# Natural forms of three weights by 32-column block loads and VectorE transposes, in place of TensorE transposes; a fixed order around the chain's head

## The chip, the cores and the metric

The kernel runs on one core of a Trainium2 chip. The metric is the device time of one execution in microseconds (us); a version is measured in several runs, and the median counts. The profile is of one execution: each instruction on TensorE (PE, and PEld for its weight loads), VectorE (DVE), ScalarE (ACT), GpSimd (POOL) and SyncE (SP, which issues most transfers), and every DMA packet.

## The reference, cut to what matters

Four layers on an image of 8 x 512 x 32 x 32, all in float32. The first layer has f, g and h as 1x1 convolutions with batch statistics, and a spectral norm for each image; the second is an attention over the 1024 points of an image.

```python
# layer 0
f = relu(batchnorm(conv1x1(x, Wf, bf)))      # 64 channels; statistics over all 8 images
g = relu(batchnorm(conv1x1(x, Wg, bg)))
h = conv1x1(x, Wh, bh)
z = einsum('bcn,bcm->bnm', f, g)             # per image
attn = z / largest_singular_value(z)
x = conv1x1(einsum('bnm,bcm->bcn', attn, h), Wv, bv) + x
# layer 1
h = group_norm(x)
q, k, v = wq @ h + bq, wk @ h + bk, wv @ h + bv        # wq, wk, wv, wp: 512 x 512
attn = softmax(q.T @ k * 512 ** -0.5)
x = x + wp @ (v @ attn.T) + bp
# layer 2: a second attention with 128 channels; layer 3: signs of x times signs of W, batch norm, PReLU
```

The kernel doesn't make q and k. It uses `q.T @ k = h.T (wq.T wk) h`, so it makes the product `wu` of the two weights once, and likewise `wo` from wv and wp. The host hands every weight over with its input channel on the partitions ("turned"); the products `wu` and `wo` need wq, wk and wv the other way round, with the output channel on the partitions. These are the natural forms of this document.

## The kernel before

**First stage (`for b in range(B)`, line 1360).** For each image its tile `xt` (2 MB, four quarters `cc` of 512 KB) is loaded on SP's queue into one of two buffers, so the load of image b waits until TensorE has read image b-2. TensorE makes f, g and h (line 1372, `bank<-xt,fg` and `bank<-xt,h`), ScalarE evicts f, VectorE evicts g and takes statistics of both (`bn_stats`). For the last two images h is left for later (`late_h`). Between the images the table `later` (line 1347) loads the other weights: w3 beside image 1, q beside 2, k beside 3, v beside 4, z and tpg beside 6, each as one DMA; the scheduler places them in SP's queue.

**Natural forms (`natural`, line 1332).** A generator. For each weight TensorE turns 16 blocks of 128x128 with the identity into two wide PSUM tiles; ScalarE and VectorE evict them, four blocks of 128 at a time. q is turned behind the last image's f and g, k around the statistics, v as the first thing that `filler` gives.

**Statistics.** Two aggregates on VectorE, then a matmul with `fold` (line 1517) for the mean over images, small VectorE work, a second matmul with `fold` (line 1523) for the variance, `rsqrt_eps` (GpSimd's power and a Newton step on VectorE), and the scale and bias of the ReLU (`relu`, line 1502, on ScalarE). Each f goes to DRAM (`f_dram`) and comes back later (`load_f`).

**Grams.** For a pair of images `turned_pair` turns f and g with TensorE (line 1266) and evicts half with VectorE, half with ScalarE; `gram` (line 1473) makes their 64x64 products.

**The chain (`first_chain`, line 1147).** The singular value of the first pair by repeated squaring: 22 steps, each two matmuls of 128x128 (lines 1159, 1160) whose evictions (one VectorE, one ScalarE) the next step needs, and in every third step a total (line 1187). Between the steps TensorE takes pieces of other work from the generator `filler` (line 1577), a fixed number for each step: first the turning of v, then the product `wu` (line 1417, 16 pieces; its first half evicted by ScalarE, its second by VectorE), the late h of two images, the grams of the other pairs with VectorE's sums of `wu` (`sums_u`) and the bias products (line 1451) among them, and last the product `wo`. The ReLUs of the other images are put on ScalarE one per step.

**Entering image 6.** Seven stages of `enter` (line 419) with 2, 2, 2, 2, 4, 3 and 6 pieces of `filler` between them: `weights0` (line 299), four visits of matmuls (line 429) that VectorE adds to x with statistics, a matmul with `gmat` (line 450), another (line 457), whose result gives the scale of h. Then h is made (`normal`, line 480), and the main part starts with line 405.

**Order.** TensorE's instructions in the loop of the chain stand under `tc.manual_schedule`: they keep the order in which the program gives them. What stands ahead of it, from the statistics to the first two grams, is ordered by the scheduler.

Of the kernel before, what the change touches and what calls it, by code (L numbers as in the profile page):

```python
# [8 lines left out]
F32 = mybir.dt.float32  # L9
# [3 lines left out]
ALU = mybir.AluOpType  # L13
# [3 lines left out]
P = 128  # L17
B = 8
C = 512
N = 1024  # L20
CC = C // P
# [39 lines left out]
COL = {n: 4 * i for i, n in enumerate(VEC512)}  # L61
# [6 lines left out]


NSTEP = 6  # L70

# [12 lines left out]
def kernel(  # L86
# [17 lines left out]
    nc = tc.nc  # L104
    mm = nc.tensor.matmul
# [11 lines left out]
    def wide():  # L117
        return psum["wide"].tile([P, N], F32, tag="wide", name="wide")
# [4 lines left out]
    def bank():  # L123
        return psum["bank"].tile([P, HF], F32, tag="bank", name="bank")
# [25 lines left out]
    sbw = {}  # L150

    def load_w(name, src, shape, pool=wpool, eng=nc.sync, tag=None):
        t = pool.tile(shape, F32, tag=tag or name, name=name)
        eng.dma_start(out=t, in_=src)
        sbw[name] = t
        return t
# [4 lines left out]
    a1 = early.enter_context(tc.tile_pool(name="a1", bufs=1))  # L161
# [32 lines left out]
    fold = fold.rearrange("p g j -> p (g j)")  # L194
# [1134 lines left out]

    nat = {}  # L1330

    def natural(name, tag):
        t = nat[name] = a1.tile([P, CC, C], F32, tag=tag, name="nat_" + name)
        for i in range(CC // 2):
            tp = wide().rearrange("p (o c j) -> p o c j", o=2, j=P)
            for k in range(2):
                for cc in range(CC):
                    nc.tensor.transpose(
                        tp[:, k, cc, :], sbw[name][:, cc, bass.ts(2 * i + k, P)], ident
                    )  # L1340
            dst = t[:, 2 * i : 2 * i + 2, :].rearrange("p o (c j) -> p o c j", j=P)
            nc.scalar.copy(dst[:, 0], tp[:, 0])
            nc.vector.tensor_copy(dst[:, 1], tp[:, 1])
            yield


    later = {
        1: [("w3", w_3, a1)],
        2: [("q", w_q, a1)],
        3: [("k", w_k, a1)],  # L1350
        4: [("v", w_v, a1)],
        6: [("z", w_z, wpool), ("tpg", w_tpg, wpool)],
    }
    shapes = {"z": [P, C], "tpg": [P, CC, 3 * P]}
# [5 lines left out]
    for b in range(B):  # L1360
        xt = load_x(b) if b else first
        for name, src, pool in later.get(b, ()):
            load_w(name, src, shapes.get(name, [P, CC, C]), pool)
        if b == 4:
            load_rows()
        if b >= B - 2:
            resident[b] = xt
        banks = [bank() for _ in w0[: 3 if b < B - 2 else 2]]

        def products(i, cc):  # L1370
            for h in range(NH):
                mm(  # L1372
                    out=banks[i][side(h), :],
                    lhsT=w0[i][:, cc, :],
                    rhs=xt[:, cc, half(h)],
                    start=cc == 0,
                    stop=cc == CC - 1,
                )

        if b == 0:  # L1380
            for cc in range(CC):
                for i in range(2):
                    products(i, cc)
        for i in range(3):
            if i == 2 and b >= B - 2:
                if b == B - 1:
                    for _ in natural("q", "w3"):
                        pass
                continue
            if b or i == 2:  # L1390
                for cc in range(CC):
                    products(i, cc)
            if i == 0:
                nc.scalar.copy(fs[b], banks[i])
                nc.vector.bn_stats(st[:, 0, b, :], fs[b])
            elif i == 1:
                nc.vector.tensor_copy(gs[b], banks[i])
                nc.vector.bn_stats(st[:, 1, b, :], gs[b])
                if last is not None:
                    turn(last[0], last[1], ht_pair[last[0] // 2], 0)  # L1400
        if b < B - 2:
            hraw = a2.tile([P, HF], F32, tag="hraw", name="hraw")
            nc.scalar.activation(hraw, banks[2], AF.Identity, bias=bhc)
            last = b, hraw
        else:
            last = None
        if b == 3:
            total3 = sign_weights()
        if b == 5:
            scale_signs(total3)  # L1410

    def product(lt, rhs, dst, vector):
        for i in range(CC // 2):
            ps = wide()
            for k in range(2):
                for oc in range(CC):
                    mm(  # L1417
                        out=ps[:, half(k)],
                        lhsT=lt[:, oc, bass.ts(2 * i + k, P)],
                        rhs=rhs[:, oc, :],  # L1420
                        start=oc == 0,
                        stop=oc == CC - 1,
                    )
                    if k == 0 or oc < CC - 1:
                        yield
            to = dst[:, 2 * i : 2 * i + 2, :].rearrange("p o c -> p (o c)")
            if i % 2 and vector:
                nc.vector.tensor_copy(to, ps)
            else:
                nc.scalar.copy(to, ps)  # L1430
            yield
# [70 lines left out]
    def relu(b, i):  # L1502
        t = (fs, gs)[i][b]
        nc.scalar.activation(t, t, AF.Relu, bias=bi0[:, i : i + 1], scale=sc0[:, i : i + 1])
        if i == 0:
            nc.sync.dma_start(out=f_dram[b], in_=t)


    mv = a1.tile([P, 2, 2], F32, tag="mv", name="mv")
    mean = a1.tile([P, 2], F32, tag="mean", name="mean")  # L1510
    dev = a1.tile([P, 2], F32, tag="dev", name="dev")
    for i in range(2):
        nc.vector.bn_aggr(mv[:, i, :], st[:, i, :, :])
    nat_k = natural("k", "q")
    next(nat_k)
    ps = bank()
    mm(out=ps[:, 0:2], lhsT=fold, rhs=mv[:, :, 0], start=True, stop=True)
    nc.vector.tensor_copy(mean, ps[:, 0:2])
    nc.vector.tensor_tensor(dev, mv[:, :, 0], mean, ALU.subtract)
    nc.vector.tensor_tensor(dev, dev, dev, ALU.mult)  # L1520
    nc.vector.tensor_tensor(dev, dev, mv[:, :, 1], ALU.add)
    ps = bank()
    mm(out=ps[:, 0:2], lhsT=fold, rhs=dev, start=True, stop=True)
    sc0 = rsqrt_eps(a1, ps[:, 0:2], 2, "r0")
    bi0 = a1.tile([P, 2], F32, tag="bi0", name="bi0")
    m0 = a1.tile([P, 2], F32, tag="m0", name="m0")
    c0 = COL["L0_conv_bf"]
    bias, gamma, beta = (ct[:, c0 + 2 * i : c0 + 2 * i + 2] for i in range(3))
    nc.vector.tensor_tensor(sc0, sc0, gamma, ALU.mult)
    nc.vector.tensor_tensor(m0, mean, bias, ALU.add)  # L1530
    nc.vector.tensor_tensor(bi0, bias, m0, ALU.subtract)
    nc.vector.tensor_tensor(bi0, bi0, sc0, ALU.mult)
    nc.vector.tensor_tensor(bi0, bi0, beta, ALU.add)
    jl = order[0] // 2
    for i in range(2):
        for k in range(2):
            relu(2 * jl + k, i)
    next(nat_k)

    def sums_u():  # L1540

        a11, a12, a21, a22 = quarters_of(wu, chunks, cols2)
# [34 lines left out]
    def filler():  # L1577

        yield from natural("v", "k")
        load_w("p", w_p, [P, CC, C], a1, tag="v")
        yield from product(nat["q"], nat["k"], wu, True)
        for b in order[:2]:
            yield from late_h(b)
        yield from gram(jl, 2, ht_pair[jl], gtl)
        scale_z()
        yield
        between = biases()
        sums = sums_u()  # L1590
        for j in rest:
            for _ in grams(j):
                next(sums, None)
                yield
                if next(between, None):
                    yield
        yield from product(nat["v"], sbw["p"], wo, False)

    todo = filler()
    for _ in range(5):  # L1600
        next(todo)
    for ftl, gtl in turned_pair(jl):
        pass
    for i, t in ((0, ftl), (1, gtl)):
        for _ in gram(jl, i, t, t):
            next(todo)

    relus = iter([(2 * j + k, i) for j in rest for i in range(2) for k in range(2)])
    with tc.manual_schedule(engines={mybir.EngineType.PE}):
        steps = entering(0)  # L1610
        for k, _ in enumerate(first_chain(jl)):

            for _ in range(4 if k == 3 * NSTEP + 3 else 2 if k % 3 == 1 or k == 0 else 1):
                next(todo, None)
            for args in (next(relus, None),):
                if args:
                    relu(*args)
        for n in (2, 2, 2, 2, 4, 3, 6):
            next(steps)
            for _ in range(n):  # L1620
                next(todo, None)
        for _ in todo:
            pass
# [194 lines left out]
```

## Time and profile before

| | |
|---|---|
| median of 3 runs | 1878.11 us (1877.98 to 1878.81) |
| the profiled execution, its whole time | 1878.7 us |
| its span, first to last instruction | 1876.8 us |
| granted TensorE clock | 0.999 of full speed |
| TensorE, 87.9 to 95.6 us | busy 6.80 of 7.70 us |
| TensorE, 105.0 to 150.7 us | busy 42.46 of 45.70 us |
| TensorE, 150.7 to 172.2 us | busy 21.50 of 21.50 us |
| VectorE, 38.3 to 49.4 us | busy 2.58 of 11.10 us |
| issue of x tiles 2, 3, 4, 5 on SP | at 17.19, 28.24, 39.28, 50.32 us |
| TensorE begins x tiles 3, 4, 5 | at 39.07, 50.11, 61.14 us |

The span is 1.9 us shorter than the execution's time, which holds what lies around the program. A line of a timeline has the start and the length in us, the engine, the line of the program, the operation, the tiles that it writes and reads, its shapes and how many instructions stand together; in brackets the idle time of the engine before it, and what ended it. A float32 matmul is shown as two records. A table by stretch has for each its length, the busy time of the five engines with the number of instructions, the clock, the share of the 16 DMA engines that were busy, and GB/s.

### The profile page before, as it was taken

How to read it: one execution, taken by the hardware profiler on the slowest of the kernel's cores; microseconds unless marked ns; L12 is line 12 of the kernel's file. 1: busy time of each engine (PE TensorE's matmuls, PEld its weight loads, DVE VectorE, ACT ScalarE, POOL GpSimd, SP SyncE). 2: the span in 40 equal slices, each digit the busy share in tenths (PEclk: the TensorE clock that was granted, in tenths of full speed). 3: DMA queues.
4: the chain of work that ended last, by engine and by line, in shares of the span. 5: the costliest groups of instructions: out<-in, count | busy, mean ns of one | idle time of the engine just before them, and what ended most of it. 6: DMA issues, size and time to landing. Idle time of an engine off the chain costs nothing.

```text
span 1876.8 us, 16564 instructions
## 1 busy us (share of the span) xinstructions
PE 1856.3 (99%) x6244; PEld 952.5 (51%) x6244; DVE 1118.4 (60%) x2077; ACT 545.4 (29%) x888; POOL 121.9 (6%) x109
## 2 busy tenths in 40 slices
PE   9999999999999999999999999999999999999997
PEld 3456465544645455544645455544645464544653
DVE  3347687467754777567764676457643666355447
ACT  2142221244202521244202522144202521244113
POOL 1000001100020001100020001100020001000011
PEclk9999999999999999999999999999999999999999
DMA  8420000002000200002000200001000200000001
GB/s 323 164 79 7 1 18 1 1 34 73 12 1 12 90 18 1 0 34 73 12 1 12 88 19 0 1 34 67 12 0 12 90 12 0 1 34 23 12 0 47
DMA packets 25202, 66.51 MB, mean 35 GB/s; under 512 B 3552, under 2 KB 4764, under 8 KB 24476
## 3 DMA queue, kind: packets, MB, share of 16 engines
q1 hardware_dynamic: 24188, 64.96, 9.6%
q8 instruction: 51, 0.84, 0.2%
q10 hardware_dynamic: 864, 0.43, 0.1%
q14 instruction: 35, 0.29, 0.0%
q0 software_dynamic: 64, 0.00, 0.0%
HBM read 46.44 MB, written 18.94 MB: 35 GB/s over the span
## 4 chain that ended last, share of the span: by engine, by line
PE 96%; DVE 2%; ACT 1%; DMA 0%; issue 0%; POOL 0%; DVEq 0%; ACTq 0%
PE bank L405 46%; PE bank L583 21%; PE bank L832 6%; PE bank L985 5%; PE bank L1372 4%; PE bank L684 3%; PE bank L701 3%; PE bank L429 2%; PE bank L724 1%; PE wide L1417 1%; PE bank L1053 1%; PE bank L1473 1%; PE bank L855 0%; PE quad L1266 0%; PE bank L1563 0%; PE bank L1159 0%
## 5 line engine op out<-in xcount | busy, mean ns | idle before, releaser
L583 PE MATMUL bank<-e,vt 128*128 128x512 f32 x768 | 336.2, 594 | 0.0
L583 PEld LDWEIGHTS bank<-e,vt 128*128 128x128 f32 x768 | 144.3, 190 | 172.3 <-issue 167.9
L405 PE MATMUL bank<-ut,h 128*128 128x512 f32 x384 | 178.9, 597 | 0.0
L405 PEld LDWEIGHTS bank<-ut,h 128*128 128x128 f32 x384 | 71.3, 190 | 94.7 <-issue 93.0
L405 PE MATMUL bank<-us,hs 128*128 128x512 f32 x256 | 115.6, 593 | 0.0
L832 PE MATMUL bank<-tpg 128*128 128x512 f32 x256 | 115.4, 595 | 0.0
L985 PE MATMUL bank<-e,tpg 128*128 128x512 f32 x256 | 114.7, 595 | 0.0
L356 DVE TENSOR_TENSOR e<-bank,e 128x512 f32<-128x512 f32 x96 | 66.1, 689 | 60.8 <-PE bank L405 45.1
L839 ACT ACTIVATE e<-bank 128x512 f32<-128x512 f32 x128 | 76.3, 597 | 67.0 <-PE bank L832 67.0
L350 ACT COPY e<-bank 128x512 f32<-128x512 f32 x96 | 56.2, 585 | 118.8 <-PE bank L405 118.5
L405 PE MATMUL bank<-wo,h 128*128 128x256 f32 x384 | 89.9, 384 | 0.0
L405 PE MATMUL bank<-h,wu 128*128 128x512 f32 x192 | 88.9, 594 | 0.0
L985 PEld LDWEIGHTS bank<-e,tpg 128*128 128x128 f32 x256 | 48.1, 190 | 60.4 <-issue 60.0
L236 POOL TENSOR_TENSOR r_r<-r_v,minus_half 128x4 f32<-128x4 f32 (+1 forms) x11 | 10.9, 989 | 1044.9 <-DVE r_v L235 1039.3
L405 PEld LDWEIGHTS bank<-wo,h 128*128 128x128 f32 x384 | 71.4, 190 | 12.6 <-issue 3.8
L405 PEld LDWEIGHTS bank<-us,hs 128*128 128x128 f32 x256 | 48.4, 190 | 57.5 <-issue 54.5
L844 DVE TENSOR_TENSOR esum<-esum,e 128x1024 f32<-128x1024 f32 x48 | 58.8, 1226 | 30.1 <-ACT e L839 29.9
L712 ACT ACTIVATE sg<-xt,rb 128x512 f16<-128x512 f32 x64 | 44.2, 716 | 107.9 <-DVE xt L703 105.0
L832 PEld LDWEIGHTS bank<-tpg 128*128 128x128 f32 x256 | 47.6, 190 | 55.0 <-issue 52.4
L356 DVE TENSOR_TENSOR vt<-bank,vt 128x512 f32<-128x512 f32 x48 | 33.2, 692 | 66.4 <-PE bank L405 65.5
L350 ACT COPY vt<-bank 128x512 f32<-128x512 f32 x64 | 37.3, 584 | 121.3 <-PE bank L405 121.2
L350 ACT COPY ut<-bank 128x512 f32<-128x512 f32 x48 | 28.1, 586 | 126.9 <-PE bank L405 126.9
(370 smaller groups left out, 2926.4 us busy)
## 6 DMA issues: line engine op xcount, KB each, us to landing
xt<-in_x SPq DMA_DIRECT2D x55, 512.0 KB
out<-both SPq DMA_DIRECT2D x63, 256.0 KB
rfull<-r_dram SPq DMA_DIRECT2D x15, 512.0 KB
f_dram<-f SPq DMA_DIRECT2D x8, 256.0 KB
fb<-f_dram SPq DMA_DIRECT2D x8, 256.0 KB
w<-in_w SPq DMA_DIRECT2D x1, 1024.0 KB
q<-in_w_q SPq DMA_DIRECT2D x1, 1024.0 KB
k<-in_w_k SPq DMA_DIRECT2D x1, 1024.0 KB
```

The lines of the kernel that those rows point to most:

```text
L350: nc.scalar.copy(dst, ps)
L356: nc.vector.tensor_tensor(dst, ps, u, ALU.add)
L405: mm(out=ps[:, q * w : (q + 1) * w], lhsT=lt(ka, kb, q, k), rhs=rhs(ka, kb, q, k), start=first and q == 0 and k == 0, stop=last and k == 1 ...
L583: mm(out=ps, lhsT=a[:, t, bass.ts(r_, P)], rhs=e[t], start=first and t == 0, stop=last and t == NTH - 1, skip_group_check=True,)
L684: mm(out=ps[:, i, :], lhsT=xt[:, cc, bass.ts(4 * h + i, P)], rhs=sbw["tpg"][:, cc, 2 * P : 3 * P], start=cc == 0, stop=cc == CC - 1,)
L701: mm(out=ps, lhsT=sbw["z"][:, bass.ts(oc, P)], rhs=att, start=True, stop=True)
L712: nc.scalar.activation(sg[:, cc, :], xt[:, cc, half(h)], AF.Sign, bias=rb3[:, cc : cc + 1])
L832: mm(out=ps, lhsT=pt[:, 0, bass.ts(t, P)], rhs=tt[:, 0, half(h)], start=True, stop=True,)
L839: nc.scalar.activation(e[:, half(h)], ps, AF.Exp, scale=float(P) ** -0.5)
L844: nc.vector.tensor_tensor(esum, esum, e, ALU.add)
L985: mm(out=banks[h], lhsT=gt[:, t, :], rhs=es[t][:, half(h)], start=t == 0, stop=t == NT - 1,)
L1372: mm(out=banks[i][side(h), :], lhsT=w0[i][:, cc, :], rhs=xt[:, cc, half(h)], start=cc == 0, stop=cc == CC - 1,)
```

## The change

`natural` has no TensorE work any more. q, k and v are loaded by `load_blocks`, sixteen DMAs each beside images 2, 3 and 4: DMA (q, r) reads 32 input rows and, of each group of 128 columns, 32 columns, and writes them on 32 partitions. Each run in DRAM is thus 32 numbers, 128 bytes. Four VectorE transposes for each weight (32x32 blocks, 512 numbers on each partition) then write the natural form. In the program they stand at the end of images 5, 6 and 7. In VectorE's compiled order they stand behind g's statistics of images 2 (q), 3 (k) and 4 (v). In SP's queue z, tpg and p come behind the load of image 6, p ahead of image 7.

The statistics, ReLUs, transposes and first two grams move into the manual schedule, with a fixed number of products ahead of and between them (3, 1, 5, 1, 1). `filler` begins with the product `wu`. The numbers of pieces for each step of the chain and of `enter` are as they were. ScalarE's compiled order behind the statistics is four ReLUs, the copy of half of `wu`, one ReLU, the evictions of `ft` and `gt`, two ReLUs, `gm`, three ReLUs, `gg_full`. In TensorE's compiled order no product stands between line 457 and the first of line 405.

```diff
+QUAD = 32
+GROUPS = 16
...
+    def load_blocks(name, src, tag):
+        t = sbw[name] = a1.tile([P, 4, GROUPS, QUAD], F32, tag=tag, name="blocks_" + name)
+        of = src.rearrange("(r a) c o -> r a (c o)", a=QUAD)
+        for q in range(4):
+            for r in range(4):
+                nc.sync.dma_start(
+                    out=t[bass.ts(q, QUAD), r],
+                    in_=of[r].rearrange("a (m w) -> a m w", w=P)[:, :, bass.ts(q, QUAD)],
+                )
+
     def natural(name, tag):
         t = nat[name] = a1.tile([P, CC, C], F32, tag=tag, name="nat_" + name)
-        for i in range(CC // 2):
-            tp = wide().rearrange("p (o c j) -> p o c j", o=2, j=P)
-            for k in range(2):
-                for cc in range(CC):
-                    nc.tensor.transpose(
-                        tp[:, k, cc, :], sbw[name][:, cc, bass.ts(2 * i + k, P)], ident
-                    )
-            dst = t[:, 2 * i : 2 * i + 2, :].rearrange("p o (c j) -> p o c j", j=P)
-            nc.scalar.copy(dst[:, 0], tp[:, 0])
-            nc.vector.tensor_copy(dst[:, 1], tp[:, 1])
-            yield
+        to = t.rearrange("p o (c r a) -> p r c o a", r=4, a=QUAD)
+        for r in range(4):
+            nc.vector.transpose(to[:, r], sbw[name][:, r].rearrange("p (c o) b -> p c o b", o=CC))
...
-        2: [("q", w_q, a1)],
-        3: [("k", w_k, a1)],
-        4: [("v", w_v, a1)],
...
+        if b in (2, 3, 4):
+            load_blocks(*((("q", w_q, "q"), ("k", w_k, "k"), ("v", w_v, "v"))[b - 2]))
...
-                if b == B - 1:
-                    for _ in natural("q", "w3"):
-                        pass
...
+        if b > 4:
+            natural(*((("q", "w3"), ("k", "q"), ("v", "k"))[b - 5]))
...
     def product(lt, rhs, dst, vector):
-                    mm(
+                    one = mm(
...
+                    if i + k + oc == 0:
+                        tc.keep_in_program_order(one)
...
     def filler():
-        yield from natural("v", "k")
         load_w("p", w_p, [P, CC, C], a1, tag="v")
         yield from product(nat["q"], nat["k"], wu, True)
...
     todo = filler()
-    for _ in range(5):
-        next(todo)
+    with tc.manual_schedule(engines={mybir.EngineType.PE}):
+        for i in range(2):
+            nc.vector.bn_aggr(mv[:, i, :], st[:, i, :, :])
+        for _ in range(3):
+            next(todo)
+        ps = bank()
+        mm(out=ps[:, 0:2], lhsT=fold, rhs=mv[:, :, 0], start=True, stop=True)
...
+        next(todo)
+        ps = bank()
+        mm(out=ps[:, 0:2], lhsT=fold, rhs=dev, start=True, stop=True)
...
+        for i in range(2):
+            for k in range(2):
+                relu(2 * jl + k, i)
+        for _ in range(5):
+            next(todo)
+        for ftl, gtl in turned_pair(jl):
+            pass
+        for i, t in ((0, ftl), (1, gtl)):
+            for _ in gram(jl, i, t, t):
+                next(todo)
```

More of the change, by code (lines that the diff above doesn't have):

```diff
@@ L1506, in relu @@
             nc.sync.dma_start(out=f_dram[b], in_=t)
[L1509 to L1538, printed above, removed]
     def sums_u():
@@ L1599 @@
     todo = filler()
-    for _ in range(5):
-        next(todo)
[L1602 to L1605, printed above, removed]
-            next(todo)
-    relus = iter([(2 * j + k, i) for j in rest for i in range(2) for k in range(2)])
-    with tc.manual_schedule(engines={mybir.EngineType.PE}):
+    with tc.manual_schedule(engines={mybir.EngineType.PE}):
+        mv = a1.tile([P, 2, 2], F32, tag="mv", name="mv")
+        mean = a1.tile([P, 2], F32, tag="mean", name="mean")
+        dev = a1.tile([P, 2], F32, tag="dev", name="dev")
+        for i in range(2):
[4 more added lines that the diff above has]
+        mm(out=ps[:, 0:2], lhsT=fold, rhs=mv[:, :, 0], start=True, stop=True)
+        nc.vector.tensor_copy(mean, ps[:, 0:2])
+        nc.vector.tensor_tensor(dev, mv[:, :, 0], mean, ALU.subtract)
+        nc.vector.tensor_tensor(dev, dev, dev, ALU.mult)
+        nc.vector.tensor_tensor(dev, dev, mv[:, :, 1], ALU.add)
+        next(todo)
+        ps = bank()
+        mm(out=ps[:, 0:2], lhsT=fold, rhs=dev, start=True, stop=True)
+        sc0 = rsqrt_eps(a1, ps[:, 0:2], 2, "r0")
+        bi0 = a1.tile([P, 2], F32, tag="bi0", name="bi0")
+        m0 = a1.tile([P, 2], F32, tag="m0", name="m0")
+        c0 = COL["L0_conv_bf"]
+        bias, gamma, beta = (ct[:, c0 + 2 * i : c0 + 2 * i + 2] for i in range(3))
+        nc.vector.tensor_tensor(sc0, sc0, gamma, ALU.mult)
+        nc.vector.tensor_tensor(m0, mean, bias, ALU.add)
+        nc.vector.tensor_tensor(bi0, bias, m0, ALU.subtract)
+        nc.vector.tensor_tensor(bi0, bi0, sc0, ALU.mult)
+        nc.vector.tensor_tensor(bi0, bi0, beta, ALU.add)
+        jl = order[0] // 2
+        for i in range(2):
+            for k in range(2):
+                relu(2 * jl + k, i)
+        for _ in range(5):
+            next(todo)
+        for ftl, gtl in turned_pair(jl):
[3 more added lines that the diff above has]
+                next(todo)
+        relus = iter([(2 * j + k, i) for j in rest for i in range(2) for k in range(2)])
         steps = entering(0)
```

## The prediction

> **What bounds the kernel now.** I read the page's busy shares first, then the busy times by stretch, then TensorE's own timeline around the edit, then ScalarE's, then the transfers.
>
> ```profile
> span 1876.8 us, 16564 instructions
> PE 1856.3 (99%) x6244; PEld 952.5 (51%) x6244; DVE 1118.4 (60%) x2077; ACT 545.4 (29%) x888; POOL 121.9 (6%) x109
> ...
> PEclk9999999999999999999999999999999999999999
> ```
>
> TensorE is busy 99% of the span at its full clock, so the time is its work plus its few waits. The edit touches only the first 180.4 us. Its own timeline there:
>
> ```profile
> 87.89 1.96 PE L1338 MATMUL wide<-ident,q 128*128 128x128 f32 x16
> 89.98 0.35 PE L1517 MATMUL bank<-mv,fold 128*128 128x2 f32 x2
> 90.43 1.39 PE L1338 MATMUL wide<-ident,k 128*128 128x128 f32 x10
> 91.66 0.37 PE L1523 MATMUL bank<-dev,fold 128*128 128x2 f32 x2
> 91.89 0.85 PE L1338 MATMUL wide<-ident,k 128*128 128x128 f32 x6
> 92.93 2.31 PE L1338 MATMUL wide<-ident,v 128*128 128x128 f32 x16 [0.19 <-DVE nat_k L1343]
> 95.61 2.84 PE L1417 MATMUL wide<-nat_k,nat_q 128*128 128x512 f32 x6 [0.37 <-DVE nat_v L1343]
> ...
> 104.97 0.49 PE L1159 MATMUL bank<-gg_full,gm 128*128 128x128 f32 x2 [0.25 <-ACT gg_full L1483]
> ...
> 175.02 0.28 PE L457 MATMUL bank<-dev,gmat 128*128 128x4 f32 x2
> 175.16 5.40 PE L1417 MATMUL wide<-p,nat_v 128*128 128x512 f32 x12
> 180.39 7.03 PE L405 MATMUL bank<-h,wu 128*128 128x512 f32 x16
> ```
>
> Columns are start and length in us. The three transposes fill 87.89 to 95.61; the six products behind L457 end just as the first L405 begins, so they are the cover of the chain that L457 starts.
>
> The first stage needs its transfers in time (columns: length, five engines' busy time, clock, share of the 16 DMA engines, GB/s):
>
> ```profile
> 16.20:27.30 11.10, 11.10 (x55) 5.48 (x53) 4.62 (x7) 5.66 (x10) 0.00 (x0) 1.00 0.84 330
> 27.30:38.30 11.00, 11.00 (x56) 3.74 (x54) 3.57 (x6) 1.27 (x2) 0.00 (x0) 1.00 0.84 331
> 38.30:49.40 11.10, 11.10 (x56) 3.83 (x54) 2.58 (x4) 1.27 (x2) 0.00 (x0) 1.00 0.91 291
> 49.40:60.40 11.00, 11.00 (x56) 3.75 (x52) 2.58 (x4) 1.27 (x2) 0.00 (x0) 1.00 0.74 268
> ```
>
> TensorE never waits here, yet the DMA engines are 74 to 91% busy: the stage is near a second bound.
>
> **Removed.** 48 transposes take 87.89 to 95.61, 7.72 us, less the slots of the two fold matmuls between them (0.45 and 0.23): 7.04 us, 0.56 of it waits. Twelve evictions go too (six on ScalarE at 0.59, six on VectorE at 0.69); both were beside TensorE.
>
> **The new order up to the chain.** A 128x512 product takes 0.90 us (6 in 5.40). Three stand first, 87.89 to 90.59; the means are ready at 89.83 (the last aggregate starts at 89.46 and takes 0.37), so the first fold matmul doesn't wait. From it to the second, VectorE needs 0.39 plus four small operations at 0.20, 1.2 us; its own slot and one product cover 1.35. The second stands at 91.94. From there to the first ReLU it was 3.38 us (91.66 to 95.04) with a 0.69 eviction of nat_k on VectorE inside; without it some 2.8, so 94.75. TensorE meanwhile does five products to 96.67 and the 16 transposes of f and g (1.84) to 98.5.
>
> ScalarE sets what follows. Its new sequence is four ReLUs, the copy of the first half of wu, one ReLU, and only then the eviction of ft:
>
> ```profile
> 95.04 1.52 ACT L1504 ACTIVATE f<-f,bi,r_r 128x512 f32<-128x512 f32 x2 [0.39 <-DVE bi L1533]
> 96.46 1.50 ACT L1504 ACTIVATE g<-g,bi,r_r 128x512 f32<-128x512 f32 x2
> ```
>
> Two ReLUs advance it 1.42. From 94.75: four to 97.6, the copy (1.00 in the trace, 0.95 of it in sequence) to 98.55, a fifth to 99.27, ft (0.57) to 99.85. The first gram waits 98.5 to 99.85: **1.35 us new wait**. Gram 1.08, product 0.90, gram 1.08, product 0.90 end at 103.9. ScalarE does gt to 100.4, two ReLUs to 101.85, gm 0.21, three ReLUs to 104.2, gg_full 0.21 to 104.4; the chain's first product stands at 104.65, against 104.97: **0.75 new wait**, 0.25 old. So the chain starts only 0.3 earlier, but with six products (5.4 us) more behind it.
>
> **The chain.** From its first product to its last total it was 45.7 us (104.97 to 150.70), 3.2 of it waits. Each step takes a fixed number of pieces of other work, and these now come six pieces further down the list: six products less (5.4), two grams (2.16), two groups of L1451 (2.0) and two groups of eight transposes (1.86) more: +0.6. VectorE's copy of wu (1.23) and the three sums at 0.69 now stand ahead of a chain eviction: about 1.05 of wait that a group of late_h covered; the waits for hraw fall from 0.79 to about 0.45 each, as a step now stands between; with ht (0.52) and the last diagonal (0.45) they come to 2.9. Chain: 46.0, to 150.65.
>
> **Behind the chain.** To L299 4.4 as before (155.05). L299 and two products 2.86, so the first L429 at 157.9. Its four visits are VectorE's: 3.02 each without the grams' copies among them (before, 165.79 to 168.81), first one 1.17 after L429: L450 at 171.5, against 172.20. Three products (2.82) to L457 at 174.3. Behind L457 nothing is left in the list; the six products that covered its chain have gone ahead. From L457 to h it is 3.11 (175.02 to 178.13), and 0.6 to the first piece: L405 at 178.0, **against 180.39: 2.4 us gained**. The lost cover is 3.4 of the 7.04. Later VectorE has 4.4 us free before 192.68 and 6.2 before 201.26, so that starting h nearer to its reader costs nothing more.
>
> **Transfers added.** 48 DMAs of 64 KB in place of three of 1 MB: 24,576 runs of 128 bytes. No row has a run of 128 bytes between DRAM and SBUF; the neighbours (packets, MB, share of the window's 16 engines) are the tiny packets in the first 8 us, and the 320-byte rows of cols in 7.15 to 9:
>
> ```profile
> q10 hardware_dynamic: 801, 0.42, 17.4%
> q0 software_dynamic: 64, 0.00, 0.5%
> ```
>
> ```profile
> q10 hardware_dynamic: 144, 0.04, 9.2%
> ```
>
> 0.5% of 128 us over 64 is 10 ns for a few bytes; 9.2% of 29.6 over 144, less 16 tiny ones, is 20 ns at 320 bytes; 17.4% of 128 over 801 is 27.8 ns at 524 bytes. The line between the first two gives 13.9 ns at 128 bytes; bounds 10 and 27.8. So 24,576 x 13.9 / 16 = 21.4 us of all engines (15.4 to 42.7).
>
> The DMA engines' need up to x tile 5: the four rows above make 9.3+9.2+10.1+8.1 = 36.8 us; q, k, v leave (2.4 per MB, from 97% of 35.4 to 39.9 for 1.81 MB: 7.4), z and tpg go behind x tile 6 (1 MB, 2.5): 26.9, and the blocks make it 48.3. TensorE reaches tile 5 at 61.14 and its last quarter 2.6 later; less 1.0 for landing (issue at 28.24, first bytes at 29.2) there are 62.8 - 16.2 = 46.6. So tile 5 is late by about 1.6 us: none at 10 ns, 23 at 27.8. SP is not the limit: a repeated issue takes 0.44, 7 us for sixteen in an 11 us batch (bounds 0.33 to 0.74; at 0.74 it would be 11.8 and a few us of stall). In its compiled order each issue also waits for the landing of the eighth before it; with some 2 us from issue to landing (an estimate: 1.0 to the first bytes, and as much again) that allows one in 0.25. The load of p passes tile 7 in SP's queue; it waits for the turning of v (about 62), tile 7 for TensorE at 72.4, so it costs nothing. The loads of f back from DRAM pass four of its stores, and are read 50 us later.
>
> The Trainium skill's page "DMA: Bandwidth & Descriptors" (Specifications) speaks against the change: below 512 B a transfer loses line rate, because the engine does a read-modify-write. The 320-byte rows at 20 ns against 27.8 at 524 bytes show no such floor. By the page the blocks would cost at least what 512 bytes do, and the kernel would take some 1898; by the rows 1877.
>
> **VectorE's turning.** Twelve transposes of 512 elements per partition. The rows have 203 ns for 32x32 and 236 for 64x64 (32 elements more): about 0.75 us each by that slope; sixteen times 203, 3.2 us, is the far bound, no less than 0.24 the near one. They stand four at a time behind g's statistics, where VectorE is idle 6.3 us (12.7 for two before L1395); three fit. At 3.2 they overrun by 6.5 against g's bank, which is needed again a batch later: still little.
>
> **Sum.** -2.4 + 1.6 = -0.8: span 1876.0 for 1876.8. That execution took 1878.7, the median is 1878.11; to it, **1877.3**. What a measurement here can tell from no change is about 0.2%, 3.8 us.
>
> **Rivals.**
> *Slow packets (slower).* The blocks' packets cost like the 320-byte rows, 20 ns: need 26.9 + 30.7 = 57.6, late 11.0, net +8.6: 1886.7. For: the engines already run at 91%. Against: 10 ns for tiny ones. It decides from 16.9 ns (26.9 + 1.536p = 46.6 + 6.2). At 27.8, 1898.7.
> *The cover isn't lost (faster).* If ScalarE's two waits (1.35, 0.75) and the sums' 1.05 hide, and no tile is late: 2.4 + 3.15 = 5.5, 1872.6. For: waits of ScalarE are short in the trace. Against: its order is fixed with the ReLUs ahead.
> *The turning binds (slower).* At 3.2 us a transpose g's eviction comes 6.5 - 2.1 = 4.4 late (2.1 idle before each L1397); were its bank wanted at once, three batches would lose 13.2: 1888.9. It begins at 6.3 / 4 = 1.6 us each. Against: the slope of the two rows.
>
> **How the numbers follow.** Forecast (within 0.2%) 0.45; slow packets 0.31; turning 0.04; cover not lost 0.20. Slower by over 0.2%: 0.35. The likeliest's own range is 1874.5 to 1881.5. To hold 8 in 10 it reaches down to 1872.3 and up to 1888; the 27.8 ns end, 1898, stays out.
>
> **What would show it.** TensorE's waits on xt around 61 to 64 near 1.6 us, with packets near 14 ns; waits of 1.35 and 0.75 at the first gram and the chain's first product; some 3.5 us of idle TensorE ahead of the first L405; first L405 near 178.0 plus any late tile. Wrong if waits on xt pass 6 us, or if that idle stretch is missing.

## The result, and the profile after

The changed kernel takes 1891.68 us (median of 4 runs, 1890.89 to 1892.15), the kernel before on the same chip 1878.46 (1877.98 to 1879.07): a ratio of 1.0070 (95% interval 1.0052 to 1.0087), 13.2 us slower. The forecast was 1877.3. The profiled execution took 1891.29 us, its span is 1889.5. Its page, busy shares and the chain that ended last:

```profile
span 1889.5 us, 16517 instructions
PE 1856.3 (98%) x6196; PEld 949.7 (50%) x6196; DVE 1122.5 (59%) x2083; ACT 541.7 (29%) x882; POOL 121.8 (6%) x109
...
PE 93%; SPq 3%; DVE 2%; ACT 1%; DMA 1%; issue 0%; POOL 0%; DVEq 0%; ACTq 0%
```

SP's queue, which has no share in the kernel before, now has 3% of the critical path, 2% of it the block loads (L1340). Line numbers are 2 to 4 higher than before (L405 is L407, L457 is L459, L1417 is L1420). Where the time went, by landmarks of TensorE's timelines (us from the span's start):

| | before | after | difference |
|---|---|---|---|
| end of the first stage (first transpose / first product) | 87.89 | 102.39 | +14.5 |
| the chain's first product | 104.97 | 118.72 | +13.75 |
| the chain's last total | 150.70 | 163.68 | +13.0 |
| second matmul with `gmat` (L457, L459) | 175.02 | 187.31 | +12.3 |
| first of L405, L407 | 180.39 | 191.11 | +10.7 |
| the eight behind its first sixteen | 187.26 | 200.78 | +13.5 |

The first stage loses 14.5 us; the edit wins 3.8 of them back up to L407, and then 2.8 go again within sixteen matmuls. From there to the end the difference changes by less than 1 us (the spans differ by 12.7).

**The first stage.** TensorE's timeline, the groups that waited for an x tile:

```profile
42.74 4.51 PE L1376 MATMUL bank<-xt,fg 128*64 128x512 f32 x20 [0.69 <-DMA xt<-in_x]
...
53.92 2.25 PE L1376 MATMUL bank<-xt,fg 128*64 128x512 f32 x8 [2.49 <-DMA xt<-in_x]
...
74.08 8.60 PE L1376 MATMUL bank<-xt,fg 128*64 128x512 f32 x32 [6.63 <-DMA xt<-in_x]
```

Tiles 3, 4 and 5 come late; with two smaller waits (0.49 and 1.03) it is 11.3 us. The 32 matmuls of tile 5 take 8.60 us where the later groups of 32 take 7.09: another 1.5 us, which begin at a granted clock of 0.50 (last row of the stretches below). The rest of the 14.5 us: TensorE began tile 2 at 28.27 instead of 28.03, and each of the five waits costs some 0.3 us more than its idle time. Why the tiles are late stands in SP's timeline (start, length, line, operation, tile, count):

```profile
17.43 1.76 SPq L141 DMA_DIRECT2D xt<-in_x  x4
19.23 14.58 SPq L1340 DMA_DIRECT2D blocks_q<-in_w_q  x16
33.92 1.98 SPq L141 DMA_DIRECT2D xt<-in_x  x4
35.94 13.39 SPq L1340 DMA_DIRECT2D blocks_k<-in_w_k  x16
49.44 2.08 SPq L141 DMA_DIRECT2D xt<-in_x  x4
51.56 14.89 SPq L1340 DMA_DIRECT2D blocks_v<-in_w_v  x16
...
69.22 4.44 SPq L141 DMA_DIRECT2D xt<-in_x  x8
```

Sixteen issues take 13.4 to 14.9 us, not 7. The next x tile stands behind them, so tiles 3, 4 and 5 are issued at 33.92, 49.44 and 69.22; before, it was 28.24, 39.28 and 50.32. The chain of waits has the single issues (start, length):

```profile
21.37 1.52 SPq L1340
22.94 3.50 SPq L1340
26.49 0.63 SPq L1340
```

Most take 0.62 or 0.63 us, with the next one 0.67 after; the fourth and fifth behind an x tile take 1.5 and 3.5. 14 x 0.67 + 5 = 14.4. That is the prediction's far bound ("at 0.74 11.8 and a few us of stall"), not its value. Meanwhile the DMA engines are not full (last columns: TensorE's granted clock, of which 1.00 is full speed, share of the 16 engines, GB/s):

```profile
16.20:27.30 11.10, 11.10 (x54) 5.43 (x51) 4.39 (x7) 5.51 (x10) 0.00 (x0) 1.00 0.83 257
27.30:38.30 11.00, 11.00 (x54) 3.78 (x52) 4.86 (x8) 1.42 (x3) 0.00 (x0) 1.00 0.74 157
38.30:49.40 11.10, 10.41 (x50) 3.40 (x48) 4.12 (x8) 1.27 (x2) 0.00 (x0) 1.00 0.82 185
49.40:60.40 11.00, 6.90 (x30) 1.68 (x28) 2.61 (x4) 1.20 (x2) 0.00 (x0) 1.00 0.90 241
60.40:71.40 11.00, 7.05 (x34) 2.20 (x30) 5.19 (x8) 0.76 (x2) 0.00 (x0) 0.95 0.61 110
71.40:75.50 4.10, 1.42 (x4) 0.51 (x6) 0.00 (x0) 0.00 (x0) 0.00 (x0) 0.50 0.91 308
```

Share times length makes 46.8 us of work up to 75.5, about when tile 5 is in; the prediction had 48.3. The need was right. But 59.3 us went by: the engines stood idle for 12.5, about what the tiles are late.

Shorter stretches tell where. While the fourth and fifth issue hung (21.37 to 26.45), with the x tile ahead of them still landing, the engines' share was 1.00. While SP sent the rest of the sixteen (26.45 to 33.90) it was 0.59, and 0.68 and 0.58 in the same stretches behind the next two tiles (42.00 to 49.40, 58.10 to 66.50). A block load is 512 packets, which took 13.7 ns each on average; on 16 engines that is 0.44 us (an estimate from these two numbers), and SP sends one each 0.67 us. So this pace leaves the engines a third idle, and these three stretches hold some 9 of the 12.5 us. The stall costs SP 5 us, but in a time in which the engines are full.

**Behind the chain.** Two lines of TensorE's timeline, and the stretch around the second by windows:

```profile
187.31 0.28 PE L459 MATMUL bank<-dev,gmat 128*128 128x4 f32 x2
191.11 9.84 PE L407 MATMUL bank<-h,wu 128*128 128x512 f32 x16 [3.52 <-DVE h L482]
```

```profile
188.00:191.00 3.00, 0.00 (x0) 0.00 (x0) 1.73 (x9) 0.52 (x1) 0.89 (x1) 0.80 0.00 0
191.00:194.00 3.00, 2.89 (x4) 1.38 (x5) 3.00 (x7) 0.00 (x0) 0.00 (x0) 0.50 0.02 5
194.00:197.00 3.00, 3.00 (x6) 1.21 (x5) 2.97 (x4) 0.59 (x1) 0.00 (x0) 0.56 0.00 0
```

The idle stretch of 3.5 us is there as predicted. Not predicted: the sixteen matmuls behind it take 9.84 us instead of 7.03, and the granted clock stands at 0.50 and 0.56 in these rows. VectorE, which makes h, is busy all the time too, so it might have been its pace; that needed an experiment.

### The profile page after: what moved, and what is told of

Same layout as the page of the kernel before. It is cut to its first block, busy times and chain, and to the rows that moved or that the text cites. A ratio compares the mean times of both kernels' runs of the same rounds, so it can differ in the third digit from the quotient of the medians.

```text
span 1889.5 us, 16517 instructions
## 1 busy us (share of the span) xinstructions
PE 1856.3 (98%) x6196; PEld 949.7 (50%) x6196; DVE 1122.5 (59%) x2083; ACT 541.7 (29%) x882; POOL 121.8 (6%) x109
## 4 chain that ended last, share of the span: by engine, by line
PE 93%; SPq 3%; DVE 2%; ACT 1%; DMA 1%; issue 0%; POOL 0%; DVEq 0%; ACTq 0%
PE bank L407 46%; PE bank L585 20%; PE bank L834 6%; PE bank L987 5%; PE bank L686 3%; PE bank L703 3%; SPq L1340 2%; PE bank L1376 2%; PE bank L431 2%; PE bank L726 1%; PE wide L1420 1%; PE bank L1478 1%; PE bank L1055 1%; PE bank L857 0%; PE quad L1268 0%
## 5 line engine op out<-in xcount | busy, mean ns | idle before, releaser
L407 PE MATMUL bank<-ut,h 128*128 128x512 f32 x384 | 178.9, 598 | 0.0
L407 PEld LDWEIGHTS bank<-ut,h 128*128 128x128 f32 x384 | 71.4, 190 | 94.5 <-issue 92.9
L407 PE MATMUL bank<-us,hs 128*128 128x512 f32 x256 | 115.6, 593 | 0.0
L407 PE MATMUL bank<-h,wu 128*128 128x512 f32 x192 | 91.7, 610 | 3.5 <-DVE h L482 3.5
L407 PE MATMUL bank<-wo,h 128*128 128x256 f32 x384 | 89.9, 384 | 0.0
L407 PEld LDWEIGHTS bank<-wo,h 128*128 128x128 f32 x384 | 71.5, 190 | 12.5 <-issue 3.8
L407 PEld LDWEIGHTS bank<-us,hs 128*128 128x128 f32 x256 | 48.5, 190 | 57.3 <-issue 54.4
L1376 PE MATMUL bank<-xt,fg 128*64 128x512 f32 x256 | 61.8, 627 | 15.7 <-DMA xt<-in_x 11.3
```

Source lines behind the costliest of these rows:

```text
L407: mm(out=ps[:, q * w : (q + 1) * w], lhsT=lt(ka, kb, q, k), rhs=rhs(ka, kb, q, k), start=first and q == 0 and k == 0, stop=last and k == 1 ...
L1376: mm(out=banks[i][side(h), :], lhsT=w0[i][:, cc, :], rhs=xt[:, cc, half(h)], start=cc == 0, stop=cc == CC - 1,)
```

## The experiments

The theory: SP's queue, with 0.67 us for an issue and a stall behind each x tile, holds the x tiles up. Its rivals: the DMA engines' time for the small packets; VectorE's turning or the new order. Separately: the 9.84 us are the clock, or h arriving piece by piece.

| kernel | first product | first L407 | idle before it, time of its first 16 | median us | ratio to before, 95% interval |
|---|---|---|---|---|---|
| changed | 102.39 | 191.11 | 3.52, 9.84 | 1891.68 | 1.0070 (1.0052 to 1.0087) |
| one load of 1 MB | 87.28 | 175.99 | 3.52, 9.77 | 1877.36 | 0.9988 (0.9978 to 0.9997) |
| 16 DMAs, 2 KB runs | 92.75 | 181.46 | 3.52, 8.80 | 1882.37 | 1.0015 (1.0005 to 1.0025) |
| 8 an image, on SP | 98.18 | 186.89 | 3.52, 9.87 | 1883.92 | 1.0026 (1.0016 to 1.0036) |
| on GpSimd | 100.17 | 189.52 | 3.52, 10.13 | 1890.56 | 1.0060 (1.0040 to 1.0080) |
| 8 an image, on ScalarE | 90.08 | 183.45 | 3.51, 7.10 | 1883.98 | 1.0024 (1.0014 to 1.0033) |
| unread products | 105.34 | 194.15 | none, 7.13 | 1891.65 | 1.0058 (1.0041 to 1.0075) |
| one product, not three | 103.06 | 190.21 | 1.70, 7.10 | 1888.81 | 1.0053 (1.0036 to 1.0070) |
| 512-byte runs, 8 an image | 94.26 | 182.97 | 3.52, 8.80 | 1881.45 | 1.0012 (1.0002 to 1.0021) |
| the same, one product | 93.75 | 180.88 | 1.70, 7.10 | 1878.26 | 0.9992 (0.9982 to 1.0001) |
| late v | 89.65 | 178.47 | 3.52, 9.75 | 1877.26 | 0.9986 (0.9976 to 0.9995) |
| late v, one product | 88.01 | 175.22 | 1.70, 7.11 | 1873.03 | 0.9971 (0.9960 to 0.9983) |
| the same, 512-byte runs | 88.15 | 175.29 | 1.67, 7.11 | 1872.87 | 0.9961 (0.9947 to 0.9976) |

The kernel before had medians of 1878.65 to 1879.9 beside these runs. The kernels with one load of 1 MB and with 2 KB runs leave out the order of the blocks, so that their product of the weights has other values. The chip's first matmuls start a little differently in each execution (the first 32 took 8.9 to 10.1 us), so landmarks of two kernels agree to 1 or 2 us only.

**One load of 1 MB each.** In `load_blocks`:

```diff
-        for q in range(4):
-            for r in range(4):
-                nc.sync.dma_start(out=t[bass.ts(q, QUAD), r], in_=...)
+        nc.sync.dma_start(out=t.rearrange("p r m w -> p (r m w)"), in_=src.rearrange("p c o -> p (c o)"))
```

> Each of q, k, v comes in one DMA of 1 MB with long runs, in the same place of SP's queue; everything else stands as in the changed kernel (left out: the order of the blocks, so that the product of the weights has other values). Theory (the sixteen block loads hold up SP's queue, and x tiles 3, 4 and 5 behind them): the waits on xt go, the first product stands near 87.9 us instead of 102.4, and the time falls by 14 to 15 us to about 1877. Rival (the stall comes from VectorE's transposes or from the new order): the waits stay and the time stays within 2 us of 1891.7.

The waits on xt are gone, the first product stands at 87.28, and the time falls by 14.3 us. VectorE's turning and the order, which are unchanged, aren't the cause. This kernel is also the rest of the edit by itself: its span is 1874.7, 2.1 less than before.

**The same DMAs with long runs.**

```diff
-                    in_=of[r].rearrange("a (m w) -> a m w", w=P)[:, :, bass.ts(q, QUAD)],
+                    in_=of[r].rearrange("a (m w) -> a m w", w=QUAD)[:, bass.ts(q, GROUPS), :],
```

> The same 48 DMAs of 64 KB at the same places, each from 32 runs of 2 KB instead of 512 runs of 128 bytes (left out: the order of the blocks). If what counts is the number of runs (in the issue or in the engines): an issue takes about 0.44 us, sixteen take some 7 us, x tiles come in time, about 1877. If what counts is the number of DMAs (each waits for the landing of the eighth before it, or pays a fixed cost): sixteen issues still take 13 to 15 us, and the time stays near 1891.

Neither number came: 92.75 lies between 87.28 and 102.39. SP's timeline, and its waits:

```profile
18.52 12.70 SPq L1340 DMA_DIRECT2D blocks_q<-in_w_q  x16
31.34 1.78 SPq L141 DMA_DIRECT2D xt<-in_x  x4
```

```profile
SPq L1340 <- DMA xt<-in_x: 11.8, 10, 2.7
```

An issue now takes 0.31 to 0.42 us where it isn't held up, as predicted, but ten of them waited 11.8 us in all, up to 2.7 each. These are the waits for the landing of the eighth DMA before: for the fifth to the eighth block that is a quarter of the x tile just ahead, issued at 16.7 to 18.1 us and landed at 21 to 27, 4.5 to 9 us after its issue. So of the 15.1 us some 9.6 (102.39 to 92.75) come with the 128-byte runs, and 5.5 with sixteen DMAs queued behind an x tile.

**Eight beside each of images 1 to 6.**

```diff
-        if b in (2, 3, 4):
-            load_blocks(...)
+        if 1 <= b <= 6:
+            load_blocks(..., ((0, 1), (2, 3))[(b - 1) % 2])
```

> The same 48 block loads of 128-byte runs, but eight beside each of images 1 to 6 instead of sixteen beside 2, 3 and 4. If SP's queue is the limit (0.9 us an issue): eight take some 7.5 us, which fits ahead of the next x tile that SP waits some 9 us for, and nearly all of the 14.5 us goes: 1877 to 1879. If the DMA engines' time for the 128-byte packets is the limit: up to tile 5 only a third of it has gone, tiles are late by 4 to 5 us in as many images as before: 1886 or more.

Neither: 1883.9. Eight issues took 8.5 to 11.9 us, because the stall comes with every x tile, however many blocks follow; and those beside image 1 took longest, where the DMA engines are already full (1.01 of them from 8 to 16 us), so that tile 2 was issued at 21.38 instead of 17.19.

**On GpSimd.** `nc.sync` becomes `nc.gpsimd` in `load_blocks`.

> The same 48 block loads of 128-byte runs beside images 2, 3 and 4, issued by GpSimd instead of SP. If SP's queue is what fails (the same packets leave the DMA engines time enough): x tiles are issued near 28, 39 and 50 us as before the change, the waits on xt stay under 2 us, and the time is 1877 to 1879, unless GpSimd is too slow to make 24,576 descriptors before the first product needs them (no row has its price). If the DMA engines fail: the waits on xt stay near 14 us in all, 1889 or more.

The rival's time, with waits on xt of 8.8 us in all instead of 14. GpSimd isn't too slow (0.65 us an issue), but it doesn't stand behind the x tiles: it sent all 48 blocks between 4.0 and 47.2 us, from beside tile 0 on, and filled the engines. By windows from 16 to 38 us (the share is the number before the last):

```profile
16.00:27.00 11.00, 8.44 (x36) 2.49 (x34) 1.37 (x3) 0.69 (x1) 7.86 (x13) 0.91 1.03 281
27.00:38.00 11.00, 9.77 (x44) 2.91 (x42) 5.51 (x8) 5.44 (x10) 7.94 (x13) 0.94 1.04 276
```

So the engines are a bound too, for blocks that are sent this early. It is not the same test as the budget of 48.3 us against 46.6, though: GpSimd's queue shows 1,600 packets for 3.15 MB, where ScalarE's in the next run shows 26,208 for 3.58 MB, so the packets are others.

**On ScalarE, eight an image.** As the spread above, with `nc.scalar`.

> The 128-byte block loads issued by ScalarE, eight beside each of images 1 to 6. Compared with the same spread on SP (1883.9, first product at 98.2 us). If the time is lost because blocks and x tiles stand in one queue in order: the x tiles come in time, the first product stands at 88 to 90 us, 1876 to 1879. If the packets in the DMA engines are what makes the tiles late: first product still near 98, 1883 or more. A third possibility: ScalarE's stalls hold up the evictions of f, and TensorE waits on banks instead of xt.

TensorE waits for xt only once more, 0.62 us in tile 0, so it matters whether the blocks stand in the queue of the x tiles. The time goes elsewhere: the blocks of k land late, and VectorE, which turns them in its fixed place, stands before them while g's bank and the statistics wait behind (VectorE's waits from 55 to 97 us):

```profile
DVE nat_k L1350 <- DMA blocks_k<-in_w_k: 9.0, 3, 3.9
```

Later the four turnings of v stand ahead of the second aggregate (91.94 to 95.47). TensorE waits 0.69 and 0.89 us for g and 3.03 for the aggregates. ScalarE's issues are held up as well, with no x tile in its queue: five of them took 10.0 us from 21.16 on, with the engines' share at 1.04.

**The clock, first: unread products.** Four products behind L459 into a PSUM tile that nobody reads.

```diff
+        ps = wide()
+        for k in range(4):
+            mm(out=ps[:, half(k % 2)], lhsT=nat["v"][:, k, 0:P], rhs=sbw["p"][:, k, :], start=True, stop=True)
```

> The changed kernel with four products behind L459 whose result nobody reads, 3.6 us of TensorE work in the idle stretch of 3.5 us ahead of the first L407. If that idle stretch lowers the granted clock behind it: the first sixteen of L407 take 7.0 us instead of 9.8 and the kernel gains 2 to 3 us, about 1889. Rival (the 9.8 us come from h arriving piece by piece from VectorE): they still take 9.8, and the time stays within 0.5 us of 1891.7.

The mechanism is shown by the trace:

```profile
194.15 7.13 PE L407 MATMUL bank<-h,wu 128*128 128x512 f32 x16
```

h arrives no earlier, and the sixteen take 7.13. The kernel's median did not move (1891.65; the four runs lie between 1888.02 and 1892.13): in this execution tile 5 was 7.40 us late instead of 6.63, with slow matmuls behind it (9.70 for 32), and the first product 2.95 later, which ate the 2.7.

**The clock, second: one product, not three, between L452 and L459.**

```diff
-        for n in (2, 2, 2, 2, 4, 3, 6):
+        for n in (2, 2, 2, 2, 4, 1, 6):
```

> The changed kernel with one product instead of three between L452 and L459 and nothing else. L459 comes 1.8 us earlier; if the stretch of 1.7 us leaves the granted clock alone, the first sixteen of L407 take 7.1 us instead of 9.8: 4.5 us less in all, 1887. If only the idle time counts: 1.8 us less, 1890.

The idle stretch is 1.70, the sixteen take 7.10: from L452 to the eight behind them it is 12.0 us (185.16 to 197.16) against 16.3 (184.48 to 200.78), 4.3 less. The median falls only 2.9; its first product stands 0.7 later.

**512-byte runs.** Any order of the summed index gives the same product, if both factors have it. Group q then takes 128 neighbouring columns.

```diff
-                    in_=of[r].rearrange("a (m w) -> a m w", w=P)[:, :, bass.ts(q, QUAD)],
+                    in_=src.rearrange("(r a) c o -> r a c o", a=QUAD)[r][:, :, bass.ts(q, P)],
```

> Another order of the summed index: the 32 partitions of group q take columns 128q to 128q+127 of q, k and v (and p and two bias vectors are loaded in the same order), so that each run is 512 bytes; eight DMAs of 128 runs beside each of images 1 to 6 on SP. The sums are the same up to their order. If an issue costs 0.62 us because of 512 runs and 0.42 with fewer, and a stall behind each x tile takes the rest: eight issues and the stall take under 9 us, x tiles are not late, first product at 87.3 to 89, 1876 to 1878. If the stall behind the x tile alone is enough to lose the time, the first product stays later than 92, 1882.

> The run before with one product instead of three between L452 and L459, so that two stand behind L459. Clock theory (an idle stretch of 3.5 us costs 2.7 us more in a lower granted clock behind it): L459 comes 1.8 us earlier, the idle stretch shrinks to 1.7 us, the first sixteen of L407 take 7 us: 4 to 4.5 us less than the run before, near 1872. Without the clock: 1.8 us less.

The second alternative: 94.26. Here the waits for the x tile's quarters are as in the run with 2 KB runs, and eight small loads of the two bias vectors, put ahead of tile 5, held SP for some 3.5 us more. With one product the median falls by 3.2 us (expected 4 to 4.5; the clock had dropped less in the first, 8.80).

**Late v.** q and k over images 2 to 6, v behind the load of image 7, turned beside the chain.

```diff
+SPANS = {2: (0, 6), 3: (6, 12), 4: (12, 19), 5: (19, 26), 6: (26, 32), 7: (32, 48)}
...
+        for n in range(*SPANS.get(b, (0,))):
+            load_blocks(..., [divmod(n % 16, 4)])
...
         yield from product(nat["q"], nat["k"], wu, True)
+        natural("v", "k")
         load_w("p", w_p, [P, CC, C], a1, tag="v")
```

> 128-byte runs on SP as in the changed kernel, but q and k are spread over images 2 to 6 (6, 6, 7, 7, 6 DMAs), and v comes behind the load of image 7 and is turned during the chain (its product with p is needed 75 us later). Budget theory (the DMA engines need 48.3 us of the 46.6 up to tile 5, and any time in which SP's queue keeps them idle is added): up to tile 5 the blocks now need 26/48 of 21.4 us, 38.5 us in all, and seven issues with the stall behind an x tile fit in an 11 us batch: no tile is late by more than 1 us, first product at 87.3 to 88.5, time 1877 to 1879.5. If a stall behind each x tile costs TensorE time however few blocks there are: first product at 91 or later, over 1881.

> The run before with runs of 512 bytes (group q takes columns 128q to 128q+127, p and two bias vectors in the same order), and one product instead of three between L452 and L459. First product at 87.3 to 88; idle stretch ahead of L407 1.7 us instead of 3.5, no drop of the clock behind it: 4 to 4.5 us less than with whole loads (1877.4), plus up to 1.5 us for the turning of v on VectorE beside the chain: 1873 to 1875, faster than the kernel before by 0.2 to 0.3%. If the idle stretch or the stalls come back elsewhere: 1877 or more.

> The run with late v and 128-byte runs (1877.3), with the one change behind the chain: one product instead of three between L452 and L459. If the length of the runs no longer matters once the loads are spread: idle stretch 1.7 us, first sixteen of L407 7.1 us, 4.5 us less, 1872.5 to 1873.5, like the run with 512-byte runs (1872.9). If the short runs still cost TensorE time: 1874.5 or more.

The times came as expected (1872.87 just below its range). In the first of the three the first product stood at 89.65, not at 87.3 to 88.5; its first 32 matmuls had taken 9.96 us. With the 128-byte runs, still on SP, six to seven issues take 6.8 to 8.5 us, inside the 9 or so that SP would wait for TensorE anyway (28.99, its next x tile, less 19.7); the only wait for xt left is 0.70 us in one of the two. With one product the sixteen take their 7.11:

```profile
171.32 0.38 PE L460 MATMUL bank<-dev,gmat 128*128 128x4 f32 x2
175.22 7.11 PE L408 MATMUL bank<-h,wu 128*128 128x512 f32 x16 [1.70 <-DVE h L483]
```

That version is 5.6 us faster than the kernel before (0.9971, 0.9960 to 0.9983), and 18.6 us faster than the changed one. The longer runs add nothing that can be told (1872.87 against 1873.03).

## Why the prediction was wrong

- **The step that failed: "SP is not the limit: a repeated issue takes 0.44, 7 us for sixteen in an 11 us batch".** It took 14.6. Two terms were mis-sized. An issue of 512 runs takes 0.62 (a pace of 0.67), where the 0.44 came from rows of 128 long runs: the prediction took the price of another kind of DMA and kept the true one only as a bound, without a price in its range. Its own sign of being wrong came: the waits on xt passed 6 us, with 11.3. And "some 2 us from issue to landing" held for none of the DMAs that count: the eighth before the fifth block is an x quarter, which lands 4.5 to 9 us after its issue in the run with 2 KB runs. With 128-byte runs the same place shows as an issue of 1.5 to 3.5 us; the engines are full while it lasts, and what the instruction waits for the trace does not say.
- **The budget was right, its premise wrong.** 48.3 us of need were 46.8. Tile 5 was to be 1.6 late if the engines never stopped; they stood idle for 12.5 us, most of it because SP sent a block load each 0.67 us, and with no slack left an idle microsecond of theirs is a late microsecond of a tile. Packets at 13.7 ns (13.9 predicted) settle the rival of slow packets: its 1886.7 was nearer to the result than the forecast, by a mechanism that didn't occur. The prediction read the line on 512 bytes of the Trainium skill's page "DMA: Bandwidth & Descriptors" (Specifications) as a floor in the time of a packet, which would have made it 1898. No such floor is seen: 13.7 ns for 128 bytes, 27.5 for the 768 packets of 512 bytes in the kernel before. That the rate falls, as the page says, is seen in the same numbers: 9 bytes a ns against 19. The blocks themselves gained little from 512-byte runs, as their packets took over 40 ns on average.
- **VectorE's turning**: 0.71 us against 0.75, three to four of them beside TensorE. Right; that rival is dead.
- **The order and the lost cover**, read from the kernel with one load of 1 MB: L407 4.4 us earlier (predicted 2.4), 0.6 of that from its earlier start. The first gram waited 1.11 (1.35 predicted), the chain's first product 0.25 and no more (0.75 new predicted); the chain took 44.9 (46.0), its waits 1.4 instead of 2.9. The idle stretch, 3.52, is as predicted. Missing was its second price: 2.7 us at half the clock. The two errors nearly cancel, which is luck: span -2.1, predicted -2.4.

So with the loads out of the way the forecast for the rest was near by luck, and the miss of 14.4 us is one queue: with whole loads the kernel takes 1877.36.

## What to carry to other kernels

Price an issue from a row with the same number of runs, and ask of a queue in order not only how long its issues take but what lands ahead of them: a load that others wait for must not stand behind many small ones. Ask too whether the queue's pace keeps the DMA engines busy. Where their budget has no slack, spread small loads over the batches and move what isn't needed yet (here v, whose product begins at 154.3 us) out of the stage; that was worth 14 us. Longer runs helped as long as sixteen loads stood together (1882.37 against 1891.68), and added nothing once they were spread with v moved. When work is taken off the busiest engine, leave cover for the last chain: an idle stretch near 3.5 us cost 1.7 to 3.0 us beyond itself in seven of eight kernels, one of 1.7 nothing.

## What the runs showed of the hardware

- **The clock behind an idle stretch.** In eight kernels TensorE stood idle for 3.51 or 3.52 us ahead of L407. Seven times the next sixteen matmuls took 8.80 to 10.13 us, once (the loads on ScalarE) 7.10. With 1.67 or 1.70 us idle it was 7.10 or 7.11 in all four, and 7.13 with work in the gap. The Trainium skill's page "TensorE: Matmul & The Clock Gate", Part 1, has the reason: the clock halves after an idle window of about 3.4 us, and the window runs freely, so it matters where the gap falls in it. The traces agree on the window: in the changed kernel the clock changes at 70.32, 77.14, 189.78 and 196.61 us, whole multiples of 3.41 apart. They differ on "idle", since a window wholly inside a gap of 3.52 would be rare. TensorE was busy for 1.22 us of the window from 186.37 to 189.78, and the clock fell at its end, 2.2 us after L459 had ended. With the loads on ScalarE the gap lay across two windows, busy 1.68 and 1.63 us, and the clock stayed; in the four kernels with 1.67 or 1.70 us idle the window that holds the gap is at least half busy. Counted so in the kernels of the table above, a full clock fell to half behind every window with TensorE busy for up to 0.42 of it, and behind none at 0.46 or more. Two idle gaps of 0.59 and 1.97 us in one window were enough (blocks on GpSimd, at 24.94). The prediction had the gap and didn't apply the page.
- **The price of an issue on SP**, not held up: 0.31 to 0.42 us for 32 runs of 2 KB, 0.56 for 128 runs of 512 bytes, 0.62 for 512 runs of 128 bytes. On GpSimd 0.65 for the last, which its queue moved in fewer and larger packets.
